# Two images at a time in spatial halves, the convolution on four 64x64 tiles, half-width transfers on two queues

## The chip, the cores and the metric

The kernel runs on one core of a Trainium2 chip. The metric is the device time of one execution in microseconds (us). The profile's span, the stretch that its slices and chains cover, is 1.6 to 1.9 us shorter than that time. Most executions of one kernel agree within about half a per cent here. Some fall in a slower state (in e6b_act_queue 126.85 to 127.30 us, against 124.50 for its fast run); each is marked fast or slow, and only fast ones are compared unless the text says otherwise.

## The reference

It computes x + convolution(group norm(x)), for x of shape (8 images, 32 channels, 128, 128) in fp32. Cut to what matters:

```python
fx = fft2(pad(gn(x), 256 x 256), norm='ortho')      # gn: 16 groups of 2 channels
wf = fft2(pad(weight, 256 x 256), norm='ortho')     # weight: (32, 32, 3, 3)
sp = ifft2(einsum('bihw,oihw->bohw', fx, wf), norm='ortho').real
out = x + sp[:, :, 64:192, 64:192] + bias
```

The crop begins at (64, 64), so only rows and columns 62 to 127 of the normalized image are read, and only rows and columns 0 to 65 of the output receive anything from the convolution. Elsewhere the output is x + bias.

## The kernel before

Four images (4 x 32 channels) lie on the 128 partitions. Each transfer carries a band of rows of four images and is 128 partitions wide; all of them are issued by the sync engine.

```python
CHUNKS = ((0, 24), (24, 24), (48, 20), (68, 32), (100, 28))
for grp in range(NGRP):                                       # two groups of four images
    src = x[grp * IMGS : (grp + 1) * IMGS].rearrange("b c h w -> (b c) h w")
    for i, (r0, rows) in enumerate(CHUNKS):
        xt = xpool.tile([P, rows, W], F32, ...)
        nc.sync.dma_start(xt, src[:, r0 : r0 + rows, :])
```

Per group come 32 statistics instructions (4 rows each), a few small instructions for the moments of channel pairs, the normalization into `g`, and the convolution: nine taps for every six output rows, with the 32x32 weights block-diagonal in a 128x128 matrix, of which three quarters are zeros.

```python
for r in range(0, nrc, BLOCK):                                # BLOCK = 6 output rows
    ps = ps_conv.tile([P, BLOCK, NC], F32, ...)
    for a in range(K):
        for b in range(K):
            nc.tensor.matmul(ps, w_bd[:, a * K + b, :],
                g[:, top : top + BLOCK, left : left + NC], start=..., stop=...)
    nc.vector.scalar_tensor_tensor(part, in0=ps, scalar=bias_sb, in1=part, ...)  # x + conv + bias
    if grp + 1 < NGRP:
        take_stats(grp + 1, ...)                              # next group's statistics meanwhile
nc.sync.dma_start(dst[:, r0 : r0 + rows, :], xt)
```

## Time and profile before

| | before |
|---|---|
| time, median of the first 3 runs | 187.21 us (186.94 to 187.78) |
| profiled span | 185.6 us |
| matrix engine (PE) busy | 137.0 us, 74% |
| vector engine (DVE) busy | 61.1 us, 33% |
| bytes moved | 33.76 MB, mean 182 GB/s over the span |

In the prediction below you find the page's slices, the chain and the groups of this kernel. The rate of all transfers in 40 slices of 4.6 us:

```profile
GB/s 177 231 351 446 422 425 426 432 432 308 328 407 113 4 230 109 0 0 0 170 170 0 0 212 74 396 452 0 0 42 297 0 0 4 0 339 0 0 15 267
```

Between the fourth and the ninth slice the transfers run at 422 to 446 GB/s; later they stop again and again, since there is nothing to move. The kernel before has transfer time to spare.

### The profile page before, as it was taken

To read this page: it belongs to the slowest core of one execution; us is meant where nothing else is said; L and a number is where in the kernel's file an instruction comes from. 1 tells how busy PE (TensorE), PEld (TensorE's weight loads), DVE (VectorE), ACT (ScalarE), POOL (GpSimd) and SP (SyncE) were. 2 spreads that over 40 slices of the span, in tenths; PEclk is the share of its full clock that TensorE was granted. 3 is DMA by queue.
4 is the path that set the end of the run, shared out by engine and by line. 5 is a ranking of instruction groups with operands and counts; after the bars stand their busy time and mean duration, and the time that the engine had idled before them with its cause. 6 is when DMAs were issued, how large, how long until landed. Compare 5 with 4: busy or idle time off the path is not lost.

```text
span 185.6 us, 1044 instructions
## 1 busy us (share of the span) xinstructions
PE 137.0 (74%) x404; PEld 78.0 (42%) x404; DVE 61.1 (33%) x102; ACT 25.8 (14%) x16; POOL 5.2 (3%) x17
## 2 busy tenths in 40 slices
PE   0000000249999999999999929999999999999960
PEld 0000000225555555555555515555555555555530
DVE  0258799599779611101110062101110011101110
ACT  0050200379700000000000029500000000000000
POOL 4230000000000000000000000000000000000000
PEclk9999999999999999999999996999999999999997
DMA  5689999997792052000440051990007000080006
GB/s 177 231 351 446 422 425 426 432 432 308 328 407 113 4 230 109 0 0 0 170 170 0 0 212 74 396 452 0 0 42 297 0 0 4 0 339 0 0 15 267
DMA packets 3268, 33.76 MB, mean 182 GB/s; under 512 B 576, under 2 KB 704, under 8 KB 704
## 3 DMA queue, kind: packets, MB, share of 16 engines
q1 hardware_dynamic: 2880, 33.56, 43.4%
q10 hardware_dynamic: 384, 0.15, 0.4%
q8 instruction: 3, 0.05, 0.1%
q14 instruction: 1, 0.01, 0.0%
HBM read 16.93 MB, written 16.78 MB: 182 GB/s over the span
## 4 chain that ended last, share of the span: by engine, by line
PE 74%; DMA 11%; DVE 9%; issue 1%; SPq 0%; ACT 0%; ACTq 0%
PE ps L192 73%; DMA x<-x_dram 11%; DVE stats L113 6%; DVE g L158 2%; DVE x L200 1%; DVE mv L132 1%; PE ps_v L147 1%; SPq L72 0%; PE ps_m L137 0%; ACT std L150 0%; DVE var L143 0%; DVE rstd L152 0%; DVE mean L139 0%; DVE diff L141 0%; ACT L150 0%
## 5 line engine op out<-in xcount | busy, mean ns | idle before, releaser
L192 PE MATMUL ps<-g,w_bd 128*128 128x396 f32 x396 | 135.4, 504 | 6.7 <-DVE g L158 6.7
L192 PEld LDWEIGHTS ps<-g,w_bd 128*128 128x128 f32 x396 | 76.3, 193 | 64.7 <-issue 9.9
L200 DVE SCALAR_TENSOR_TENSOR x<-ps,bias_sb,x 128x396 f32<-128x396 f32 x22 | 13.9, 630 | 103.2 <-PE ps L192 103.2
L113 DVE BATCH_NORM_STATS2 stats<-x 128x6 f32<-128x512 f32 x64 | 39.0, 679 | 12.3 <-DMA x<-x_dram 12.3
L137 PE MATMUL ps_m<-mv,pair 128*128 128x1 f32 x4 | 0.8, 278 | 32.8 <-DVE mv L132 32.8
L137 PEld LDWEIGHTS ps_m<-mv,pair 128*128 128x128 f32 x4 | 0.9, 250 | 33.1 <-issue 32.8
L175 ACT ACTIVATE x<-x,bias_sb 128x256 f32<-128x256 f32 (+2 forms) x6 | 14.5, 2483 | 0.0
L171 ACT ACTIVATE x<-x,bias_sb 128x1488 f32<-128x1488 f32 (+1 forms) x6 | 8.5, 1429 | 8.3 <-DVE stats L113 6.4
L150 ACT ACTIVATE std<-ps_v,eps 128x1 f32<-128x1 f32 x2 | 0.5, 261 | 59.6 <-PE ps_v L147 59.6
L158 DVE TENSOR_SCALAR g<-x,mean,rstd 128x396 f32<-128x396 f32 (+2 forms) x6 | 5.8, 1032 | 0.0
L150 ACT ACT_TABLE_LOAD x1 | 1.3, 1283 | 15.8 <-PE ps_v L147 15.8
L147 PE MATMUL ps_v<-var,pair 128*128 128x1 f32 x4 | 0.9, 304 | 2.8 <-DVE var L143 2.8
L171 ACT ACT_TABLE_LOAD x1 | 1.3, 1283 | 9.1 <-DMA bias_sb<-bias_dram 9.1
L132 DVE BATCH_NORM_AGGREGATE mv<-stats 128x2 f32<-128x192 f32 x2 | 2.0, 1022 | 0.1
L147 PEld LDWEIGHTS ps_v<-var,pair 128*128 128x128 f32 x4 | 0.8, 249 | 3.0 <-DVE var L143 1.7
L86 POOL COPY w_bd<-w_sb 32x288 f32<-32x288 f32 x4 | 1.7, 421 | 5.1 <-DMA w_sb<-weight_dram 5.0
L152 DVE RECIPROCAL rstd<-std 128x1 f32<-128x1 f32 x2 | 0.3, 164 | 2.5 <-ACT std L150 2.5
L83 POOL MEMSET w_bd<- 128x1152 f32 x1 | 1.1, 1058 | 0.3 <-POOLq L224 0.3
L95 POOL TENSOR_SCALAR_AFFINE_SELECT pair<-pair 128x128 f32<-128x128 f32 x1 | 0.7, 706 | 0.1
L91 POOL TENSOR_SCALAR_AFFINE_SELECT pair<-pair 128x128 f32<-128x128 f32 x1 | 0.7, 706 | 0.0
L139 DVE COPY mean<-ps_m 128x1 f32<-128x1 f32 x2 | 0.3, 153 | 0.7 <-PE ps_m L137 0.7
L143 DVE SCALAR_TENSOR_TENSOR var<-diff,mv 128x1 f32<-128x1 f32 x2 | 0.4, 212 | 0.0
(9 smaller groups left out, 1.9 us busy)
## 6 DMA issues: line engine op xcount, KB each, us to landing
x<-x_dram SPq DMA_DIRECT2D x4, 1536.0 KB, 13.9
out_dram<-x SPq DMA_DIRECT2D x4, 1536.0 KB, 5.1
x<-x_dram SPq DMA_DIRECT2D x2, 2048.0 KB, 22.3
out_dram<-x SPq DMA_DIRECT2D x2, 2048.0 KB, 8.2
x<-x_dram SPq DMA_DIRECT2D x2, 1792.0 KB, 24.9
out_dram<-x SPq DMA_DIRECT2D x2, 1792.0 KB, 6.6
x<-x_dram SPq DMA_DIRECT2D x2, 1280.0 KB, 17.9
out_dram<-x SPq DMA_DIRECT2D x2, 1280.0 KB, 4.4
```

What stands on the lines that cost most here:

```text
L83: nc.gpsimd.memset(w_bd, 0.0)
L86: nc.gpsimd.tensor_copy(w_bd[part, :, part], w_sb[part])
L113: nc.vector.bn_stats(all_stats[grp][:, s0 + r // RSTAT, :], xts[grp][i][:, r : r + RSTAT, :].rearrange("p h w -> p (h w)"),)
L132: nc.vector.bn_aggr(mv, stats.rearrange("p n s -> p (n s)"))
L137: nc.tensor.matmul(ps_m, pair2, mv[:, 0:1], start=True, stop=True)
L147: nc.tensor.matmul(ps_v, pair2, var, start=True, stop=True)
L150: nc.scalar.activation(std, ps_v, AF.Sqrt, bias=eps, scale=float(FFT * FFT))
L158: nc.vector.tensor_scalar(g[:, lo - LO : r0 + rows - LO, 0:N], xt[:, lo - r0 : rows, LO:W], mean, rstd, ALU.subtract, ALU.mult,)
L171: nc.scalar.activation(xt[:, 0:nrc, NC:W], xt[:, 0:nrc, NC:W], AF.Identity, bias=bias_sb)
L175: nc.scalar.activation(xt[:, nrc:rows, :], xt[:, nrc:rows, :], AF.Identity, bias=bias_sb)
L192: nc.tensor.matmul(ps, w_bd[:, a * K + b, :], g[:, top : top + BLOCK, left : left + NC], start=(a == 0 and b == 0), stop=(a == K - 1 and b ...
L200: nc.vector.scalar_tensor_tensor(part, in0=ps, scalar=bias_sb, in1=part, op0=ALU.add, op1=ALU.add)
```

## The change

The matrix engine's array is to be used as four 64x64 tiles at once instead of as one 128x128 matrix of which a quarter is useful. Two images (64 channels) fill the rows of a tile. So each pair of images is split in space: the upper partitions hold other rows of the same two images than the lower ones. Tile (i, j) takes its input from partition half i and writes to partition half j, and the four work on different output rows. Eight images are four pairs in place of two groups, and the first pair can begin after half as many bytes. The halves are filled by transfers of 64 partitions, one issued on the sync engine's queue, one on the queue of GpSimd, another engine of the core. The order of instructions is fixed by hand. The diff, cut to its core (names and removed lines shortened where "..." stands, some lines joined):

```diff
-            nc.sync.dma_start(xt, src[:, r0 : r0 + rows, :])
+    queues = (nc.sync, nc.gpsimd)
+    for pair in range(NPAIR):
+        xt = xpool.tile([P, HROWS, W], F32, name=f"x{pair}")     # HROWS = 2 * 17 + 30
+        for j, queue in enumerate(queues):
+            queue.dma_start(in_quarters(xt, j), quarters(x, pair, j))   # 64 partitions, 34 rows
+        for j, queue in enumerate(queues):
+            queue.dma_start(in_lower(xt, j), lower(x, pair, j))         # 64 partitions, 30 rows
...
-                        nc.tensor.matmul(ps, w_bd[:, a * K + b, :],
-                            g[:, top : top + BLOCK, left : left + NC], ...)
+                for i in range(2):
+                    for j in range(2):
+                        top = Q * j + r + K - 1 - a + 4 * i
+                        nc.tensor.matmul(
+                            ps[HP * j : HP * (j + 1), i, 0 : rows * NC],
+                            w_bd[HP * i : HP * (i + 1), a * K + b, :],
+                            g[HP * i : HP * (i + 1), top : top + rows, left : left + NC], ...)
...
+    for pair in range(NPAIR):
+        ps = multiply(pair, 0)                       # SPLIT = ((0, 6), (6, 6), (12, 5)) rows
+        if not last: take_stats(pair + 1, 0, 9)
+        add(pair, 0, ps)
+        ps = multiply(pair, 1)
+        if not last: take_stats(pair + 1, 9, NSTAT); ps_m = moments(pair + 1)
+        add(pair, 1, ps)
+        ps = multiply(pair, 2)
+        if not last: normalize(pair + 1, ps_m)
+        add(pair, 2, ps)
+        for j, queue in enumerate(queues):
+            queue.dma_start(quarters(out, pair, j), in_quarters(xts[pair], j))
+        if not last: store_lower(pair + 1)
...
-    with tile.TileContext(nc) as tc:
+    with tile.TileContext(nc) as tc, tc.manual_schedule():
```

A channel's moments now have to be averaged over both partition halves and two channels; that takes one small matmul per pair instead of two per group.

## The prediction

> **What bounds the kernel now.** I read the page's busy shares and slices first, then the chain that ended last, then the groups, then the waits, then the queue's own waits.
>
> ```profile
> PE 137.0 (74%) x404; PEld 78.0 (42%) x404; DVE 61.1 (33%) x102; ACT 25.8 (14%) x16; POOL 5.2 (3%) x17
> ...
> PE   0000000249999999999999929999999999999960
> ...
> DVE  0258799599779611101110062101110011101110
> ...
> PEclk9999999999999999999999996999999999999997
> DMA  5689999997792052000440051990007000080006
> ```
>
> In 40 slices of 4.6 us, PE (matrix engine) is full from slice 9 to slice 38 with one dent. Before slice 9 it does nothing; DMA and DVE (vector engine) are full there. So the kernel has two halves in sequence: 40 us of load and statistics, then two solid PE stretches.
>
> ```profile
> 8.87 13.71 DMA x<-x_dram
> ...
> 22.60 9.01 DVE stats L113 x15
> ...
> 39.83 67.76 PE ps L192 x198
> ...
> 111.71 67.66 PE ps L192 x198
> ```
>
> These lines of the chain in order of time (start, length, what) say that the two convolutions are 67.7 us each and nothing else in them matters: 73% of the span. What is not PE is 39.8 us ahead, 4.1 us between and 6.2 us behind (185.6 span).
>
> ```profile
> L192 PE MATMUL ps<-g,w_bd 128*128 128x396 f32 x396 | 135.4, 504 | 6.7 <-DVE g L158 6.7
> L192 PEld LDWEIGHTS ps<-g,w_bd 128*128 128x128 f32 x396 | 76.3, 193 | 64.7 <-issue 9.9
> L113 DVE BATCH_NORM_STATS2 stats<-x 128x6 f32<-128x512 f32 x64 | 39.0, 679 | 12.3 <-DMA x<-x_dram 12.3
> L200 DVE SCALAR_TENSOR_TENSOR x<-ps,bias_sb,x 128x396 f32<-128x396 f32 x22 | 13.9, 630 | 103.2 <-PE ps L192 103.2
> ```
>
> Each of the 198 matmul calls is two records. The 504 ns is a modelled length; successive records start 332 ns apart at full clock (660 ns for the first five, so a cold start costs 1.6 us). 396 columns in 332 ns is 0.84 ns per column per record. The statistics overlap at their ends too: 15 in 9.01 us is 0.60 us each, not 0.679. The wait column of the last line shows the vector engine idle for 103 us, waiting for PE.
>
> ```profile
> SPq L72 <- DMA x<-x_dram: 9.4, 2, 6.8
> ```
>
> From the DMA queue's own waits: the second load was held back 6.8 us behind an earlier transfer, and the records show nothing moving around 8 us. Part of the slow start is that hole.
>
> [...] This trace has only the full array[...]; it does show a weight load starting 2 ns after a matmul on the same rows, so loads overlap running matmuls.
> [...] All of the kernel's large transfers are 128 wide here and run at 425 to 432 GB/s when not held[...]. This is my largest doubt.
> [...]
>
> **The change part by part.**
>
> *Matmuls.* Four images block-diagonal on the whole array use a quarter of it. Two images on 64 rows use half of a tile, and four tiles work on different row ranges. Calls per pair of images: 3 row splits x 9 taps x 4 tiles = 108, or 216 records in 54 rounds of four. If the four of a round truly overlap, a round costs what one record costs: 18 rounds of 396 columns (332 ns, 5.98 us), again 18 (5.98 us), and 18 of 330 columns (277 ns, 5.0 us). A pair is 16.95 us; four pairs 67.8 us instead of 135.4. One after the other they would cost four times that, 271 us. A round holds eight PE instructions, 41 ns each; the trace does not show whether PE issues that fast, and its shortest cold two-load, two-matmul sequence (the tiny statistics matmul) starts four records in 237 ns. Unscaled that would be 118 ns per load and matmul, 472 per round[...].
>
> *Vector engine.* Per pair: 16 statistics x 0.60 = 9.6; aggregate 1.02; a few tiny ones 0.15 each; three chained squares 0.6; square root on ACT and reciprocal 0.55; normalization 2.0 (from 1377 ns per 2112 elements and 479 per 396); six adds 3.4. About 17.5 us against 16.95 of PE. What was idle two thirds of the time is now as loaded as PE, and its order is fixed. Count from the start of a pair's first split: last adds of the previous pair 1.1, nine statistics 5.4 (6.5), two adds 1.2 (7.7), seven statistics 4.2 (11.9), aggregate and scaling 1.2 (13.1). The moments matmul sits on PE ahead of the third split, whose predecessors are done at 11.96. So PE stands about 1.2 us for the vector engine, then 0.6 us for the small full-array matmul[...], and runs the third split 13.8 to 18.8. Meanwhile the vector engine adds (1.2) and normalizes (about 3.4) by 18.3, in time. A period is therefore about 18.9 us, for three of the four pairs.
>
> *Start.* Instead of 8.4 MB, the first pair is 4.2 MB, and the sync queue's issues are no longer held. The ramp of before reaches full rate about 4 us in; at 430 GB/s quarters would land at 8 us and the lower part at 12.6. The catch is on GpSimd: the eight loads that it issues stand ahead of the masks, and the vector engine waits for the masks before its first statistic. [...]statistics start at 11 to 12 us and end near 21.5. Aggregate, matmul, squares, root, reciprocal and the large normalization add 1.2 + 0.6 + 0.75 + 0.35 + 0.2 + 1.75. PE starts between 23 (quick issue) and 27; I take 25, where it was 39.8. The early root removes the 1.28 us table load from that path.
>
> *End.* The last pair has no statistics to wait for: 17.2 us, adds 1.2. Then 2.2 MB of stores. Before, 1.31 MB took 4.45 us to land, 3.0 at rate and 1.4 fixed, and closing took 1.1. Now 5.2 to 7 at rate + 2 + 1.1: about 9 us.
>
> *Elsewhere.* ACT (scalar engine) has 3840 and 2108 elements a pair, some 5.6 us: beside other work. The removed second table load and small weight transfers lay off the path.
>
> *Sum.* 25.0 + cold 1.6 + 3 x 18.9 + 17.2 + 1.2 + 9.2 = 110.9 us of span. The measured time was 1.6 us above the span (187.2, 185.6): 112.5; I say **113 us**, 40% less.
>
> **The rivals.**
>
> *Half-width transfers become the bound.* 33.5 MB at 430 GB/s is 78 us, hidden. At half rate, some 215 GB/s, it is 156 us, and time would be near 158. [...] Against: [...]here both queues hold work all the time, so engines may spread over both halves. Between: at 290 GB/s traffic is 116 us, the backlog outlasts PE, and time is about 121; at 350 it is about 114.
>
> *The tiles do not fully overlap.* At 400 ns per round a pair takes 21 us, the vector engine's wait goes, and time is about 121. At 500 it is 143. With only two tiles at a time (664) four pairs cost 136 us of matmul and the time is about 180, level with before. Four in sequence, 300. For: twice the weight loads per column streamed, and issue untested. Against: the weight load hides today at 193 of 332 ns with twice the columns.
>
> *PE and vector engine interlock better or worse.* Without the 1.9 us stall per pair, quick GpSimd issue and full-rate stores, the time is 103. If small vector operations cost more, each extra 1 us per pair costs 3 us.
>
> **Range and chances.** I centre on overlapping tiles and mildly impaired transfers. Down to 104 if everything goes well; up to 132 for either impairment at moderate strength. Transfers at half rate (about 1 in 10) or poor tile overlap lie beyond, and only the latter reaches the old time. Faster by over 2%: 0.94. Within 2%: 0.02. Slower: 0.04.
>
> **What would show it.** Right: matmul records starting four to a round of about 332 ns; PE busy from about 25 us; three short PE idles per profile put down to the vector engine at the moments matmul; vector engine about 65 us busy; loads done by 45 to 60 us. Wrong: rounds well over 400 ns with weight-load or issue gaps; PE waiting for loads in the second, third or fourth pair; a DMA share full to the end of the span with GB/s near 215; the first statistic waiting for GpSimd far past 12 us; a final store well over 9 us.

## The result, and the profile after

| | before | after |
|---|---|---|
| time, median | 187.49 us (186.94 to 187.78, 4 runs) | 125.19 us (124.65 to 125.84, 4 runs) |
| profiled span | 185.6 us | 123.6 us |
| PE busy | 137.0 us | 72.1 us |
| DVE busy | 61.1 us | 70.1 us |
| mean rate over the span | 182 GB/s | 274 GB/s |

The ratio is 0.668 (95% interval 0.665 to 0.671). A ratio in this document is the mean time of one kernel's fast runs over that of the other's of the same rounds, so it is not quite the ratio of the medians. The output is correct.

The slices of the page after, 3.1 us each (a digit is the busy share in tenths; PEclk is the clock granted to PE, DMA the busy share of the 16 transfer engines):

```profile
PE   0000000000149999899998999997999999920000
...
DVE  1620008769699489869999869999860303030000
...
PEclk9999999999999999999999999999999999995555
DMA  3999999999999999999999999999999999989991
GB/s 87 237 226 249 243 285 239 222 260 249 245 276 249 224 259 242 272 249 270 254 241 396 289 355 431 425 406 399 369 327 241 266 280 365 345 236 241 231 217 48
```

Compare the DMA line with that of before: it no longer has any holes. The transfer engines are busy from the second slice to the last but one, while PE begins in slice 11 and ends in slice 36. And "busy" does not mean "at full rate": the GB/s line stands near 250 from the second slice to the twenty-first, reaches 399 to 431 for four slices, and falls back to 217 to 241 at the end. The final 5s of PEclk belong to an idle PE and explain nothing.

The groups show that the work per instruction is what it was:

```profile
L214 PE MATMUL ps<-g,w_bd 64*64 64x396 f32 (+1 forms) x864 | 70.5, 484 | 3.5 <-DVE g L187 3.5
L156 DVE BATCH_NORM_STATS2 stats<-x 128x6 f32<-128x512 f32 x64 | 38.8, 678 | 13.9 <-DMA x<-x_dram 13.9
```

864 matmul records are busy for half the time that 396 took. In the trace the four records of a round start within 30 ns of one another, and the next round follows 332 ns after the last: exactly the interval at which single full-array records followed each other before. So four tiles work in the time of one.

The chain that ended last, in order of time (start, length, what), shows where the first third of the span went:

```profile
2.07 23.79 DMA x<-x_dram
25.88 4.86 DVE stats L156 x8
...
35.75 7.99 PE ps L214 x72
43.76 1.17 DVE x L228 x2
44.93 4.17 DVE stats L156 x7
...
86.72 22.16 PE ps L214 x288
108.91 0.56 DVE x L228
```

The first pair's loads are not complete before 25.9 us; the first multiplication starts at 35.75, only 4 us earlier than before (39.83), although the first pair is half as large as the first group was. Three stretches and their rates (columns: stretch in us and its length, busy time of PE, of PE's weight loads, of DVE, ACT and POOL with the number of instructions, granted clock, DMA share, GB/s; ACT is the scalar engine, POOL is GpSimd):

```profile
8.00:60.00 52.00, 24.49 (x276) 12.11 (x280) 34.59 (x69) 11.36 (x6) 2.49 (x8) 1.00 1.02 253
74.00:90.00 16.00, 15.36 (x194) 7.26 (x190) 15.33 (x31) 4.62 (x3) 1.14 (x2) 1.00 1.01 403
108.90:123.60 14.70, 0.00 (x0) 0.00 (x0) 1.03 (x2) 0.00 (x0) 0.61 (x1) 0.57 0.77 186
```

Loads move at 253 GB/s with all engines busy; stores in the middle at 403; and 14.7 us pass after the last multiplication, most of it for 2.2 MB of stores. Which queue moves at a time can be read from the transfers of a short stretch, by queue (packets, MB, share of the 16 engines' time; q1 is the sync queue and carries partitions 0 to 63, q0 the GpSimd queue with 64 to 127). First 76 to 82 us:

```profile
DMA packets 279, 2.54 MB, mean 423 GB/s; under 512 B 47, under 2 KB 47, under 8 KB 47
...
q1 hardware_dynamic: 138, 1.37, 53.8%
q0 software_dynamic: 140, 1.16, 46.4%
```

and then 112 to 116 us, in the final stores:

```profile
DMA packets 96, 0.82 MB, mean 205 GB/s; under 512 B 2, under 2 KB 2, under 8 KB 2
...
q1 hardware_dynamic: 94, 0.82, 96.2%
q0 software_dynamic: 2, 0.00, 0.1%
```

Where stores of both halves are under way at once, they move 423 GB/s; where all engines serve one half, 205, and 222 from 117 to 121 us, when it is GpSimd's half. At the end the two halves go one after the other (the last packets of sync's half end at 117.5 us, of GpSimd's at 122), although both were issued between 110 and 111 us. So in these stores one half alone moved about half of what both moved together (205 and 222 of 423 GB/s). Loads are another matter: both queues have packets under way, and still only 253.

### The profile page after: what moved, and what is told of

It is laid out like the page before. It is cut to its first block, busy times and chain, and to the rows that moved or that the text cites. A ratio compares the mean times of both kernels' runs of the same rounds, so it can differ in the third digit from the quotient of the medians.

```text
span 123.6 us, 2036 instructions
## 1 busy us (share of the span) xinstructions
PE 72.1 (58%) x872; PEld 35.0 (28%) x872; DVE 70.1 (57%) x141; ACT 24.4 (20%) x14; POOL 12.0 (10%) x29
## 4 chain that ended last, share of the span: by engine, by line
PE 34%; DVE 31%; DMA 19%; issue 3%; POOL 1%; POOLq 1%; DVEq 0%; ACT 0%
PE ps L214 33%; DVE stats L156 23%; DMA x<-x_dram 19%; DVE x L228 4%; DVE mv L164 2%; PE ps_m L167 1%; DVE g L187 1%; DVE mv L165 1%; POOL x L90 1%; DVE m L176 1%; POOLq L288 1%; DVEq L288 0%; ACT std L182 0%; DVE m L173 0%; DVE rstd L184 0%
## 5 line engine op out<-in xcount | busy, mean ns | idle before, releaser
L214 PE MATMUL ps<-g,w_bd 64*64 64x396 f32 (+1 forms) x864 | 70.5, 484 | 3.5 <-DVE g L187 3.5
L214 PEld LDWEIGHTS ps<-g,w_bd 64*64 64x64 f32 x864 | 33.6, 136 | 37.9 <-issue 29.2
L228 DVE SCALAR_TENSOR_TENSOR x<-ps,wb_sb,x 128x396 f32<-128x396 f32 (+1 forms) x24 | 13.4, 601 | 16.9 <-PE ps L214 16.9
L167 PE MATMUL ps_m<-mv,avg 128*128 128x5 f32 x8 | 1.7, 289 | 33.3 <-DVE mv L165 33.3
L196 ACT ACTIVATE x<-x,wb_sb 128x3840 f32<-128x3840 f32 x4 | 14.0, 3497 | 9.8 <-DVE g L187 9.8
L187 DVE TENSOR_SCALAR g<-x,m,rstd 64x396 f32<-64x396 f32 (+2 forms) x12 | 8.6, 714 | 0.4
L256 POOL DMA_DIRECT2D out_dram<-x x4 | 2.4, 612 | 64.8 <-DVE x L228 64.8
L198 ACT ACTIVATE x<-x,wb_sb 128x2108 f32<-128x2108 f32 x4 | 8.2, 2038 | 0.0
L202 POOL DMA_DIRECT2D out_dram<-x x4 | 2.2, 541 | 32.9 <-ACT x L196 32.9
L176 DVE SCALAR_TENSOR_TENSOR m<-m 128x1 f32<-128x1 f32 x12 | 2.6, 219 | 0.4
L90 POOL DMA_DIRECT2D x<-x_dram x4 | 2.5, 622 | 0.8 <-POOLq L282 0.8
L164 DVE BATCH_NORM_AGGREGATE mv<-stats 128x2 f32<-128x96 f32 x4 | 2.4, 589 | 0.1
L92 POOL DMA_DIRECT2D x<-x_dram x4 | 2.1, 532 | 0.0
```

Source lines behind the costliest of these rows:

```text
L90: queue.dma_start(in_quarters(xt, j), quarters(x, pair, j))
L164: nc.vector.bn_aggr(mv[:, 0:2], stats[pair].rearrange("p n s -> p (n s)"))
L167: nc.tensor.matmul(ps_m, avg, mv, start=True, stop=True)
L176: nc.vector.scalar_tensor_tensor(m[:, 1:2], in0=m[:, k : k + 1], scalar=m[:, k : k + 1], in1=m[:, 1:2], op0=ALU.mult, op1=ALU.add,)
L187: nc.vector.tensor_scalar(dst, src, m[part, 0:1], rstd[part], ALU.subtract, ALU.mult)
L196: nc.scalar.activation(low, low, AF.Identity, bias=bias_sb)
```

## The experiments

Each was timed beside the kernel before on the same chip (187.4 to 187.9 us), so the ratios compare. Views come from one profiled run each. Two theories stood at first. **Width**: the missing 12.7 us of span came from half-width transfers, at the start (loads) and at the end (stores). **Rivals**: the GpSimd queue was slow or late, the order of the queues was wrong, or the vector engine and PE held each other up.

### Do the four tiles really overlap, and why? (e3_tile_by_tile)

```diff
-        for a in range(K):
-            for b in range(K):
-                for i in range(2):
-                    for j in range(2):
+        for i in range(2):
+            for j in range(2):
+                for a in range(K):
+                    for b in range(K):
```

> The changed kernel with the same 864 matmul records issued tile by tile (nine taps of one tile, then of the next) instead of the four tiles in turn. Theory (the gain on the matrix engine is overlap of neighbours in issue order that lie on different tiles): records start 332 ns apart instead of four in 332, matmuls take some 271 us and the time is 310 to 335 us, worse than before the change. Rival (a smaller tile streams faster by itself, or the engine looks ahead over matmuls): time stays near 125 us.

Correct, 283.8 us in its one run (state unknown), less than the 310 to 335 expected. The chain shows a pair's 216 records, all in one piece:

```profile
86.55 54.88 PE ps L214 x216
```

They take 54.9 us, against some 17 us in the order of the change. Same tiles, same instructions, same bytes; only the order differs. So the overlap comes from neighbouring records going to different tiles. Here the order is worth a factor of 3.2 and not four: at a switch from one tile to the next, some four of 18 records still started together with those of the neighbouring tile. This kernel, tiled but walked tile by tile, is slower than with no tiling at all (283.8 against 187.5 us).

### The same bytes in 128-partition transfers (e1_wide, then e1b_wide_wb)

Both give a wrong result: the tiles are loaded with rows of four images instead of halves of two, so that each transfer is 128 partitions wide, with the compute instructions unchanged.

```diff
-        for j, queue in enumerate(queues):
-            queue.dma_start(in_quarters(xt, j), quarters(x, pair, j))
-        for j, queue in enumerate(queues):
-            queue.dma_start(in_lower(xt, j), lower(x, pair, j))
+        nc.sync.dma_start(xt[:, 0 : 2 * Q, :], wide(x, pair, 0, 2 * Q))
+        nc.gpsimd.dma_start(xt[:, 2 * Q :, :], wide(x, pair, 2 * Q, LH))
```

and the stores likewise.

> The changed kernel with every large transfer made 128 partitions wide (same bytes per pair, still two queues: the 34-row part on one, the 30-row part on the other). Wrong results on purpose: the rows of a tile come from four images. My theory, half-width transfers cost the time: traffic runs at 400 to 430 GB/s instead of about 245, the first pair is in by 13 us instead of 25.9, the matmuls start near 24 us instead of 35.8, the last store takes 6 to 8 us instead of 12, and the time is about 108 us against 125. Rival, two queues disturb each other or the ramp is slow whatever the width: traffic stays near 245 GB/s and the time stays within 3 us of 125.

113.81 us (113.56 to 114.06), ratio 0.607 (0.605 to 0.610), against 0.668 of the change. Loads ran at 431 GB/s. The start was spoiled by a new wait, which the vector engine's waits name:

```profile
DVE w_bd L108 <- DMA wb_sb<-wb_dram: 10.6, 1, 10.6
```

The weights' small transfer, on the scalar queue, landed at 12.0 us instead of 3.1, behind the wide loads, and the vector engine's statistics stood behind the building of the weights. So I put the weights first on the sync queue:

```diff
+    wb_sb = cpool.tile([P, K * K * C + 1], F32, name="wb_sb")
+    nc.sync.dma_start(wb_sb, wb)
     xts = []
...
-    nc.scalar.dma_start(wb_sb, wb)
```

> As the full-width kernel (wrong on purpose), with the weights loaded ahead of x on the same queue. There the weights landed at 12.0 us instead of 3.1 and held the vector engine until 15.1 us. Theory (that wait, not the transfer of x, kept its matmuls from starting at 24 us): weights in by 4 us, statistics from 12 us or earlier, matmuls from 24 to 26 us, time 108 to 110 us against 113.8. Rival (x itself comes late): matmuls still start near 29 us and the time stays at 113 to 114.

Two fast runs, 109.64 and 111.26 us (two slow ones, 111.33 and 113.08), ratio 0.588 (0.584 to 0.593). Its chain and the rate from 6 to 40 us:

```profile
11.51 9.60 DVE stats L162 x16
...
26.11 7.66 PE ps L219 x72
...
76.76 22.17 PE ps L219 x288
```

```profile
6.00:40.00 34.00, 14.20 (x146) 6.63 (x146) 25.69 (x51) 5.73 (x3) 1.05 (x5) 1.00 1.01 429
```

The multiplications start at 26.11 us instead of 35.75 (9.6 less), take 72.8 instead of 73.1 until 98.9, and the rest takes 9.0 instead of 14.7 (5.7 less). Together that is 15.7 us, exactly the difference of the profiled spans, 123.6 and 107.9. The middle hardly moves. That is the width theory's picture: the loss lies at both ends. Three other things differ from the change: the place of the weights, the order of rows, and half as many transfers, each twice as large. In the change itself the weights were in by 3.1 us and held up the vector engine for only 1.7; for the size, see the loads of e10_four_images below.

### Both halves on one queue (e2_one_queue)

```diff
-    queues = (nc.sync, nc.gpsimd)
+    queues = (nc.sync, nc.sync)
```

> The changed kernel with both halves of every transfer on the sync queue. Theory (a half-width transfer alone is held to some 206 GB/s, as the trace showed while one queue was alone): 33.5 MB take 163 us, DMA share full to the end, time 165 to 172 us. Rival (switching between queues is what costs): transfers run at over 400 GB/s and the time falls below 115 us. If a second queue is useless[...], the time stays at 125.

130.23 us in its only fast run (the profiled one, 132.26, was slow), far from the 165 and more that I had expected. The rates while loads come, and late among the stores:

```profile
8.00:80.00 72.00, 42.21 (x490) 20.53 (x494) 49.73 (x95) 16.47 (x9) 0.00 (x0) 1.00 1.02 216
100.00:124.00 24.00, 12.52 (x164) 5.96 (x156) 3.37 (x6) 0.17 (x1) 0.00 (x0) 0.85 1.00 398
```

For loads one queue gives 216 GB/s (206 was expected), against 253 with two: the second queue is worth 17%. But the same half-width stores ran at 398 on that one queue. In the trace the completions of a late store are spread over 6 to 7 us (an early load's over about 1 us), while one such transfer alone takes some 5 (1.11 MB at 205 to 222 GB/s): the transfer engines had drifted apart, so at any moment some were on one transfer and others already on the next, which belongs to the other half. That this drift makes the rate is my reading and not shown: by slices of 3.3 us the stores ran at 420 GB/s from 82 us, at 278 to 382 from 85 to 104, and only then at 389 to 432. A detail against my reading of the start: here the first pair was complete at 23.4 us and PE started at 33.3, 2.4 us *earlier* than in the change, at a lower rate. By then some 4.7 MB had moved (202 GB/s over 23.4 us), only 0.3 to 0.4 MB more than the first pair and the weights, an estimate from that rate; in the change 1.11 MB of the second pair had landed before the first pair was complete.

### Storing the last pair's upper rows in thirds (e4_thirds)

```diff
         add(pair, 0, ps)
+        if last:
+            store_piece(pair, 0)        # these rows only; likewise after splits 1 and 2
```

> The changed kernel, but the last pair's upper rows are stored in three pieces, each right after its adds. Correct results. Theory (the end is long because 2.2 MB of half-width stores begin only after the last add and the two queues run one after the other, 11 us at 206 GB/s): the end after the last matmul falls from 14.7 to 7 to 10 us and the time to 118 to 121 us. Rival (the transfer engines are full to the end with earlier stores, so the order of the last ones changes nothing): time within 1.5 us of 125.

124.27 us (123.91 to 124.43), ratio 0.663 (0.661 to 0.665): about 1 us gained where I had hoped for 4 to 7. The page's DMA slices say why:

```profile
DMA  4999999999999999999999999999999999999960
```

No room was left. The engines were already full before the last pair's rows were ready; issuing earlier only lengthens the queue. My theory missed, and the rival that I had named held: what counts at the end is the whole backlog.

### An extra small transfer against lockstep (e5_tiny)

I suspected that with loads the 16 engines stay in step, all on one half at a time, and that shifting some of them would let the halves add up as they do with stores.

```diff
+        if pair == 0:
+            tiny = cpool.tile([P, 1], F32, name="tiny")
+            nc.sync.dma_start(tiny[0:8, :], wb[0:8, 0:1])
```

> The changed kernel with one more transfer of eight partitions by one word, put on the sync queue behind the first pair's upper rows. Theory (lockstep: all 16 engines turn to the same half at the same time[...]; the one-queue run moved loads at 213 GB/s and later stores at 410 with the same half widths, so width alone is not the limit): the small transfer runs on only some of the engines, puts them one packet out of step, and loads from 8 us on go from about 245 GB/s to 350 or more; first pair in by 17 to 21 us, time 112 to 118 us. Rival (half-width loads are slow whatever the phase, only stores can be fast): rate of the loads stays at 235 to 255 GB/s and the time within 1.5 us of 125.

125.42 us, ratio 0.668 (0.666 to 0.671): the same. It did put the engines out of step: a sync-queue load's completions, 0.7 us apart in the change (15.12 to 15.80), were now 1.6 us apart (15.59 to 17.18). Yet the loads kept their rate:

```profile
10.00:60.00 50.00, 24.32 (x276) 11.98 (x280) 33.79 (x64) 11.37 (x6) 1.73 (x3) 1.00 1.01 250
```

My theory of lockstep fell, and the kept traces settle it for more than this shift. From 10 to 60 us some 16 packets, as many as engines, are in flight at a time; in the change 12 or more of them belonged to one half in 69% of that time, in e5_tiny in only 24%, as rarely as in the change's stores from 74 to 90 us (22%, at 403 GB/s). So the change's loads do lean to one half at a time, but spreading them as evenly as the stores did not make them faster.

### Contiguous memory on the other side (e8_flat_source)

Its output is wrong, which doesn't matter for the time. The loads stay half-width on the chip, but each reads one contiguous piece of memory.

```diff
-            queue.dma_start(in_quarters(xt, j), quarters(x, pair, j))
+            queue.dma_start(in_quarters(xt, j), flat(pair, 0, j).rearrange(...))
...
-            queue.dma_start(in_lower(xt, j), lower(x, pair, j))
+            queue.dma_start(in_lower(xt, j), flat(pair, 1, j))
```

> The changed kernel with its half-width loads as they are on the chip's side (same partitions, same queues, same row lengths) but each read from one contiguous piece of memory instead of 64 rows at a pitch of 64 KB. Wrong results on purpose. The small extra transfer spread each load's completions from 0.7 to 1.6 us and left the rate at 250 GB/s, so my lockstep explanation has fallen. Theory now (the limit is on the chip's side[...]): loads stay at 235 to 260 GB/s, time within 2 us of 125. Rival (the limit is on the memory's side, in which rows the engines read at the same time): loads run above 350 GB/s, first pair in by 15 to 18 us.

126.75 us (two runs), ratio 0.675 (0.672 to 0.679). The loads:

```profile
10.00:60.00 50.00, 23.68 (x256) 11.54 (x260) 31.92 (x61) 9.61 (x6) 1.18 (x2) 1.00 1.00 236
```

236 GB/s, no better. So the pattern of rows in memory is not what holds the loads down. What this run and the change have in common, and e1b_wide_wb has not, is the 64-partition side on the chip (with it, twice as many transfers of half the size; but e10_four_images below loads at 426 GB/s with 128-partition transfers of 0.8 to 1.6 MB, and these are 1.0 to 1.1 MB, so size alone is not it).

### The scalar queue in place of GpSimd's (e6_act_queue, e6b_act_queue)

```diff
-    queues = (nc.sync, nc.gpsimd)
+    queues = (nc.sync, nc.scalar)
```

> The changed kernel with the scalar engine's queue in place of GpSimd's. In the changed kernel the second queue's first packet came at 7.3 us, 5.3 us behind the first queue's, though issued at 1.4 us, just as the first queue's first transfer ended. Theory A (the engines had already taken up the first queue's whole transfer): the same delay here, second queue from 6.5 to 8 us, time 122 to 128. Theory B (the GpSimd path starts slowly): second queue's packets from 3 us or earlier, first pair in by 21 us. Loads stay near 245 GB/s in both.

179.99 us, but for another reason than the one I was after: the weights were now ninth on the scalar queue. The vector engine's waits:

```profile
DVE w_bd L104 <- DMA wb_sb<-wb_dram: 72.7, 1, 72.7
```

As a test of GpSimd's queue this is confounded in the total, though not in the rate: 244 GB/s from 10 to 60 us. One queue again started late, but now it was sync's: its first packet came at 6.35 us, 4 us after the scalar queue's. I repeated it with the weights first on the sync queue, the same edit as in e1b.

> The run with the scalar engine's queue again, with the weights loaded first on the sync queue: in the last one they stood behind nine loads and landed at 74 us, which says nothing of queues. Theory (a GpSimd queue or a scalar queue is the same to the transfers): loads at 235 to 255 GB/s, second queue's first large packet some 4 to 6 us behind the first's, first pair in by 23 to 27 us, time 122 to 128 us. Rival (the GpSimd queue is the slow one): first pair in by 20 us or earlier and time below 120 us.

Its only fast run took 124.50 us; three slow ones took 126.85 to 127.30. In the profile, of a slow run, loads ran at 248 GB/s. The scalar queue's first packet came at 2.38 us and the first of x on the sync queue at 7.29, against 2.42 (sync) and 7.39 (GpSimd) in the change. So neither the rate nor the 5 us by which one queue starts late is GpSimd's doing: the late one can be sync's own.

### All statistics ahead of the first two adds (e7_adds_late)

The lines of the edit, some of them joined here:

```diff
-        ps = multiply(pair, 0)
-        take_stats(pair + 1, 0, 9); add(pair, 0, ps)
-        ps = multiply(pair, 1)
-        take_stats(pair + 1, 9, NSTAT); ps_m = moments(pair + 1); add(pair, 1, ps)
+        ps0 = multiply(pair, 0)
+        ps = multiply(pair, 1)
+        take_stats(pair + 1, 0, NSTAT); ps_m = moments(pair + 1)
+        add(pair, 0, ps0); add(pair, 1, ps)
```

> The changed kernel with the vector engine doing all 16 statistics and the moments of the next pair before the first two adds of this one, so that the matrix engine does not stand at the moments matmul. Theory (transfers are busy from 2 to 122 us and set the end): the stand of about 1 us in each of three pairs shrinks below 0.6, the last matmul ends 1.2 to 2 us earlier, and the time stays within 0.6 us of 125.2. Rival (the matrix engine's chain sets the end, as the chain of the profile says): the time falls by 1.2 to 2 us.

124.14 us (122.77 to 125.03, 6 runs, one of them slow), ratio 0.659 (0.655 to 0.662). One period of it:

```profile
54.90:72.34 17.44, 17.44 (x222) 8.47 (x218) 16.51 (x32) 5.30 (x3) 1.14 (x2) 1.00 1.01 284
```

PE no longer stands: 17.44 us busy of 17.44, where a period of the change took 18.15. In the two profiles its last multiplication ended 1.9 us earlier (107.0 against 108.9; it had begun 0.3 earlier), and the span is 0.8 us shorter, 122.8, since the transfers behind took 15.8 us instead of 14.7. But the fast runs of e7 spread over 1.8 us, so one pair of profiles can't divide so small a gain: by the means of the fast runs it is 1.3 us (123.89 against 125.22), by the ratios 1.7. My theory had set at most 0.6, the rival (PE's chain sets the end) 1.2 to 2. So PE's chain does count for the end, and how much of its gain the transfers take back stays open.

### Four tiles with full-width transfers (e10_four_images)

The experiments point to a version: keep four images on 128 partitions and the transfers 128 wide, as before, and let the normalization, not the transfer, bring the other half's rows across. `g` gets two slots: slot 0 holds the images of its own partitions for the upper output rows, slot 1 those of the other half for the lower ones. Weights come first, all on the sync queue; upper rows are stored after each add. The core, shown against the change:

```diff
-        for j, queue in enumerate(queues): ...            # half-width loads
+        for r0, rows in CHUNKS:
+            nc.sync.dma_start(xt[:, r0 : r0 + rows, :], rows_of(x, grp, r0, rows))
...
+            norm(g[:, 0, a:b, 0:N], xt[:, LO + a : LO + b, LO:W], slice(0, P))
+            for d, s in ((lo, hi), (hi, lo)):             # across the halves
+                norm(g[d, 1, a:top, 0:N], xt[s, LO + HALF + a : LO + HALF + top, LO:W], s)
...
-                        top = Q * j + r + K - 1 - a + 4 * i
+                        s = int(i != j)
+                        top = r + K - 1 - a
-                            ps[HP * j : HP * (j + 1), i, 0 : rows * NC],
+                            ps[HP * j : HP * (j + 1), s, 0 : rows * N],
-                            g[HP * i : HP * (i + 1), top : top + rows, left : left + NC],
+                            g[HP * i : HP * (i + 1), s, top : top + rows, left : left + N],
...
+        for s in range(2):                                # in add(): store these rows at once
+            store(grp, HALF * s + r, rows)
```

> The four 64x64 tiles without the half-width transfers: four images at a time, every transfer 128 partitions wide on the sync queue (weights first, upper rows stored in pieces as they are added). Tiles off the diagonal get their input by normalizing across the halves; two tiles share a bank on different partitions. Correct results. Theory (the tiles give the gain and the half widths took part of it back): traffic at 420 GB/s or more when not idle, matmuls from 29 to 33 us although 8.4 MB come first, 68 to 72 us of matmul, end within 8 us of the last matmul, time 105 to 112 us. Rival (two images at a time are needed for a short start, so that the full width gains nothing): 120 us or more.

Correct, **107.59 us** (107.06 to 108.33, 5 runs), ratio 0.573 (0.570 to 0.576): 14% under the change. Its slices (2.7 us each), and the rates from 6 to 40 us, during the multiplications and behind them:

```profile
PE   0000000000029999999999999999999999999910
...
DMA  5899999999999999399999260059099999925134
```

```profile
6.00:40.00 34.00, 8.82 (x57) 6.04 (x61) 30.00 (x50) 6.16 (x3) 0.00 (x0) 1.00 1.01 426
31.73:101.44 69.71, 69.67 (x722) 36.60 (x722) 41.59 (x66) 21.68 (x7) 0.00 (x0) 1.00 0.73 296
101.44:106.40 4.96, 0.00 (x0) 0.00 (x0) 1.17 (x2) 0.00 (x0) 0.00 (x0) 0.88 0.41 159
```

Holes are back in the DMA line, and PE is busy for 69.67 of 69.71 us: PE bounds it again. It starts 4 us earlier than in the change although it waits for twice the bytes, and ends 5.0 us after its last multiplication instead of 14.7. Several things changed at once in this version, so it proves the recipe and not each part of it. It also shows that two tiles of different rows can write the same slot of an accumulation tile, on different partitions: tiles (0,0) and (1,1) both use slot 0, the four records of a round start within 20 ns of one another in 108 of 180 rounds, with the next round 330 or 385 ns later, and the result is correct.

## Why the prediction was right or wrong

The time was predicted as 113 us within 104 to 132, and came out at 125.2: the direction, the size and the range held, and the centre was 12 us too low. By the steps of the sum:

| step | predicted span | measured | off by |
|---|---|---|---|
| until the first multiplication | 25.0 us | 35.75 | +10.75 |
| multiplications, cold start included | 75.5 (1.6 + 3 x 18.9 + 17.2) | 73.1 | -2.4 |
| after the last multiplication | 10.4 (1.2 + 9.2) | 14.7 | +4.3 |
| sum | 110.9 | 123.6 | +12.7 |

- **Four tiles in the time of one** was right: rounds of four every 332 ns, and e3_tile_by_tile shows what it hangs on. Four records of 396 columns take as long as one did. That a round would keep to 332 ns, and not to the 472 of the unscaled sequence, had been my estimate.
- **The period** was right in its mechanism: PE stands each time for the moments, and the vector engine is about as loaded as PE (from 55.62 to 73.77 us, PE is busy for 17.51 us of 18.15 and the vector engine for 16.52). Its size was 18.2 us in the middle, not 18.9, since the aggregate over 96 elements took 0.60 us (I had used the 1.02 us of 192) and adds follow each other every 0.53 to 0.59 us. The vector engine was busy for 70 us, not 65. Removing the stand (e7_adds_late) shortened PE's stretch by 1.6 us (73.1 to 71.5) and brought 1.3 to 1.7 us of time, which does not contradict the predicted 3 us for each 1 us per pair.
- **The start** failed. The line that failed is "at 430 GB/s quarters would land at 8 us and the lower part at 12.6". The first pair's last transfer landed at 25.9. I had placed the danger on GpSimd's masks, which by my estimate would let statistics begin at 11 to 12 us; the masks were done at 8.05 us, and each GpSimd issue took 0.53 to 0.72 us. The first statistic instead waited 10.1 us for a load, until 19.1. Two causes can be separated by bytes, as an estimate: by 25.9 us the 4.19 MB of the first pair had landed and also 1.11 MB of the second on the sync queue, which ran ahead. At 250 GB/s the first pair alone, from 2.4 us on, would be there at 19.2; the other 6.7 us are the late second queue and the sync queue's lead. e2_one_queue supports that: lower rate, hardly a lead (0.3 to 0.4 MB by the estimate above), first pair at 23.4.
- **The end** failed in the same term: "5.2 to 7 at rate" for 2.2 MB assumes 310 to 430 GB/s. The halves were stored one after the other, at 205 and 222. e1b_wide_wb measures the same end at 9.0 us when transfers are wide.
- **Which rival came true**: the first, in its middle form. "At 290 GB/s traffic is 116 us, the backlog outlasts PE, and time is about 121" is close to what happened at 274. I had called the width of the transfers the largest doubt and put the centre on the mild side all the same. The reason I gave there, that engines would spread over both halves while both queues hold work, holds for stores (423 GB/s) and not for loads (253). The other rivals, poorly overlapping tiles and a worse interlock, did not come.
- **Its signs of being wrong**: two came true, DMA busy to the end of the span (at a mean of 274 GB/s, not 215) and a final stretch well over 9 us, and loads were done at 74.7 us, not by 45 to 60. That the range held owes little to errors that cancel: the multiplications were over-estimated by 2.4 us, against 15 us missing at the two ends.
- **Slips that changed nothing**: the vector engine was not full in the first 40 us of the kernel before (25.2 us busy, 12.3 us waiting for loads), and two tiles at a time would give about 174 us by the sum's own terms, not 180.

**What stays open**: why loads of both halves, both under way, stop at 216 (one queue) to 253 GB/s (two queues), when stores of both halves reach 398 to 423. It is not the rows in memory (e8_flat_source: 236), not the GpSimd queue (e6_act_queue: 244, e6b_act_queue: 248) and not lockstep of the engines (e5_tiny: 250). By elimination it goes with the half-width shape on the chip's side (e1b_wide_wb: 429 when wide), which is argued rather than shown for the loads alone; the mechanism was not found. Nor was it tested why one queue's first packet waits some 5 us (7.39 against 2.42 us in the change).

## What to carry to other kernels

In this kernel four 64x64 tiles multiply in the time of one if neighbouring instructions go to different tiles (a round of four every 332 ns; a pair's 216 records took 54.9 us when walked tile by tile, against some 17), so look for a layout that fills them; but keep the transfers 128 partitions wide (loads at 426 to 431 GB/s here, against 253 with 64 partitions) and let a compute instruction that runs anyway (here the normalization) move data across the halves. When a change halves the compute of a kernel, recompute its transfers with the rate of the *new* transfer shape before trusting the gain: 33.5 MB were hidden at 430 GB/s, and in half-width transfers they cost some 15 us at the two ends (e1b_wide_wb). After the change, read the DMA line beside the GB/s line: busy everywhere at well under the rate of before pointed here to the shape of the transfers, and an earlier issue of the last stores (e4_thirds) gained only about 1 us.
